# Where the context is rotated: all sixteen tiles inside layer 0's self attention, none inside layer 1's cross attention

## The chip, the core and the metric

The kernel runs on one core of one Trainium2 chip. The metric is the device time of one execution in microseconds (us). The core has a matrix engine (PE), three engines for elementwise work (DVE, ACT, POOL), and a queue, SP, that here issues nearly all DMA transfers. The engines run their own instruction streams in order and wait for one another by semaphores.

## The reference, cut to what matters

The program is a two-layer perceiver on 64 batches of 32 latents of width 256, all in fp32, with a context of 64 x 257 x 64. Each layer is cross attention, self attention and a feed-forward block, with residuals:

```python
x = x + L0_xattn(ln(x), ctx)     # stage A, causal, first 32 context rows
x = x + L0_attn(ln(x))           # stage B, 16 heads of 128, cosine similarity
x = x + L0_ffn(ln(x))            # end of B, and stage C: 4 of 16 blocks for each token
x = x + L1_xattn(ln(x), ctx)     # stage D, all 257 context rows
x = x + L1_attn(ln(x))           # stage E
x = x + L1_ffn(ln(x))            # stage F, 8 experts, one for each token
```

The change concerns what layer 1's cross attention reads. It does not use the context as it came but the context with a rotary position applied:

```python
kv_rope = kv_c * cos[None] + rotate_half(kv_c) * sin[None]     # 64 x 257 x 64
scores  = (q_r of x) . (kv_rope @ W_kr)                        # keys
ctx_c   = softmax(scores) @ kv_rope                            # values
```

kv_rope depends on the inputs alone, so it can be computed at any time before stage D reads it.

## The kernel before

The latents are 2048 rows, held in SBUF as 16 tiles of 128 rows (four batches each). In the profiled execution stage B runs from about 139 to 505 us, C to 636, D to about 985, and E and F to the end.

**The rotation.** One tile of context is four batches. `fetch(t, work)` (L694 to L704) issues ten transfers on SP: two for `rct` (the context turned, L697), four for `rrt` (the same with its halves exchanged, L698 and L699) and four for `rna` (the context not turned, in four runs of rows, L703). `rotate(t, work)` (L706 to L721) does seven POOL multiplications and additions (L710 to L712 on the turned form, L717 to L720 on the other) and three stores on SP: two of `rct` to the DRAM tensor `ctd` (L714), one of `rna` to `nad` (L721). The four SBUF tiles that this needs have one buffer each, so the fetch of the next tile starts when the stores of the last are done. In D, `rotated(t)` (through `d_context`, L1164 and L1165) loads the rotated tile from `ctd` and `nad` as `ct` and `na`, three buffers each.

**Stage B** is a loop of 17 slots, written out by hand. The order of instructions on PE, DVE, ACT and POOL is that of the program text; SP's order is set by the framework's scheduler. Slot t computes similarities of tile t (`similar`, L806 for q.k and L814 for the squared norms, which read `q2b`), the softmax (`scale`, L828 and L830; `power`; `share`, L842 and L843), the values and output projection of tile t-1 (`gather`, L853; `project`, L866), and the queries of later tiles (L775). POOL squares the queries of tile t+1 (`square`, L794, four instructions) and ends the output norm of tile t-1 (`norm_out`, L885 and L886, which wait for DVE's L884). Where this text says that slot t starts, it means the first L806 of tile t. Other pieces are hung into the slots by `at(slot, place, fn)`: keys of the next group, the choice of feed-forward blocks (`choose_best`, L607 to L620, small DVE instructions, in slots 7, 8, 11, 12, 15 and 16), and from slot 11 on the first group of the feed-forward block (`hidden`, L644 to L652; `output`, L657). In every slot SP also writes a padding block (`srt<-pad`, L136).

Before the change `rotate` is called in the even slots, for tiles 0 to 7, each followed by the fetch of the next tile.

**Stage D** is a loop over 64 batches, in this text called blocks. Only PE's order is by hand here; DVE, ACT, POOL and SP follow the framework's scheduler. Block b has scores (L1350), their maximum on DVE (L1358), the exponential on ACT (L1362), the division on DVE (L1371), the turning of the probabilities (L1387, copied by L1393, or by DVE's L1395 every fourth block), and the product with the values (L1410, which reads `na`). DVE's L1373 puts the probabilities of the last context row aside. Every fourth block has a projection (L1426). Tiles 8 to 15 are rotated in blocks 2, 6, ..., 30, in the first half of the loop. So the second half does the same PE work with no rotation beside it.

Of the kernel before, what the change touches and what calls it, by code (L numbers as in the profile page):

```python
# [15 lines left out]
NT = B * S // P  # L16
# [21 lines left out]
def bc(ap, axis, n):  # L38

    shape = list(ap.shape)  # L40
    shape.insert(axis, n)
    return ap.unsqueeze(axis).to_broadcast(shape)
# [3 lines left out]
def perceiver_kernel(ctx: ExitStack, tc: tile.TileContext, a: dict, out: bass.AP):  # L46
# [324 lines left out]
    with tc.tile_pool(name="wA", bufs=2) as work, tc.tile_pool(  # L371
# [59 lines left out]
        def power(t):  # L431
            nc.scalar.activation(sc[t], sc[t], AF.Exp)
# [258 lines left out]
    def fetch(t, work):  # L691

        ct = work.tile([P, 2, NKV], F32, tag="rct", name=f"rct{t}", bufs=1)
        rt = work.tile([P, 2, NKV], F32, tag="rrt", name=f"rrt{t}", bufs=1)  # L694
        for z in range(2):
            src = a["ctxT"][:, 4 * t + 2 * z : 4 * t + 2 * z + 2, :]
            nc.sync.dma_start(ct[64 * z : 64 * z + 64], src)  # L697
            nc.sync.dma_start(rt[64 * z : 64 * z + 32], src[32:64])  # L698
            nc.sync.dma_start(rt[64 * z + 32 : 64 * z + 64], src[0:32])  # L699
        na = work.tile([P, 4, 2, DC], F32, tag="rna", name=f"rna{t}", bufs=1)  # L700
        srcn = a["ctxN"][4 * t : 4 * t + 4].rearrange("b (p c) d -> p b c d", c=3)
        for c, p0, r, k0, n_k in RUNS:
            nc.sync.dma_start(na[p0 : p0 + n_k, :, c, :], srcn[k0 : k0 + n_k, :, r, :])  # L703
        fetched[t] = ct, rt, na  # L704

    def rotate(t, work):  # L706
        ct, rt, na = fetched.pop(t)
        nt = work.tile([P, 4, 2, DC], F32, tag="rnt", name=f"rnt{t}", bufs=1)
        mul = nc.gpsimd.tensor_tensor
        mul(ct, ct, bc(cosT, 1, 2), ALU.mult)  # L710
        mul(rt, rt, bc(sinT, 1, 2), ALU.mult)
        mul(ct, ct, rt, ALU.add)  # L712
        for z in range(2):
            nc.sync.dma_start(  # L714
                ctd[:, 4 * t + 2 * z : 4 * t + 2 * z + 2, :], ct[64 * z : 64 * z + 64]
            )
        mul(nt[:, :, :, 0:32], na[:, :, :, 32:64], bc(sinN[:, :, 0:32], 1, 4), ALU.mult)  # L717
        mul(nt[:, :, :, 32:64], na[:, :, :, 0:32], bc(sinN[:, :, 32:64], 1, 4), ALU.mult)
        mul(na, na, bc(cosN, 1, 4), ALU.mult)
        mul(na, na, nt, ALU.add)  # L720
        nc.sync.dma_start(nad[:, 4 * t : 4 * t + 4], na)  # L721
# [4 lines left out]
    with tc.tile_pool(name="wB", bufs=2) as work, tc.tile_pool(  # L726
# [34 lines left out]
        def query_part(n_):  # L761

            pair, h2 = divmod(n_, NH // 2)
            if pair >= NT // 2:
                return
            if h2 == 0:
                queries[pair] = work.tile([P, NH, 256], F32, tag="qT", name=f"qTb{pair}")
            qT = queries[pair]
            xT = latT[pair // 2]
            c0 = 256 * (pair % 2)  # L770
            q_ps = ps2.tile([P, 2, 256], F32, tag="mm", name=f"qb{pair}_{h2}")
            for hh in range(2):
                h = 2 * h2 + hh
                for k in range(KC):
                    nc.tensor.matmul(  # L775
                        q_ps[:, hh, :],
                        b_q[:, k, h * P : (h + 1) * P],
                        xT[:, k, c0 : c0 + 256],
                        start=(k == 0),
                        stop=(k == KC - 1),  # L780
                    )
            hsl = slice(2 * h2, 2 * h2 + 2)
            nc.scalar.copy(qT[:, hsl, :], q_ps)  # L783
# [42 lines left out]
        def scale(t):  # L826
            s_ps, rq = sims[t]
            nc.vector.reciprocal(rq, rq)  # L828
            pT = sims[t] = work.tile([P, 512], F32, tag="pT", name=f"pTb{t}")
            nc.vector.tensor_tensor(pT, s_ps, rq, ALU.mult)  # L830
# [97 lines left out]
        def ff_late():  # L928
            for fn in late:
                fn()  # L930
            late.clear()
# [32 lines left out]
        for t in range(NT + 1):  # L964


            parts = [AHEAD + 4 * t + z for z in range(4)]

            def place(z):
                if z < 4:  # L970
                    query_part(parts[z])
                for step in steps.get((t, z), ()):
                    step()

            if t < NT:
                similar(t)
            place(0)
            if t > 0:
                gather(t - 1)
            if t < NT:  # L980
                scale(t)
            place(1)
            square(t + 1)
            ff_late()
            place(2)
            if t < NT:
                power(t)
            ff_late()
            place(5)
            if t > 0:  # L990
                project(t - 1)
                norm_stats(t - 1)
            if t < NT:
                share(t)
            place(3)
            ff_late()
            if t > 0:
                norm_out(t - 1)
            if t % 2 == 0 and t < NT:
                rotate(t // 2, work)  # L1000
                if t // 2 + 1 < NT // 2:
                    fetch(t // 2 + 1, work)
            if t == NT - 3:
                rotate_last()
            place(4)
            write_pad(t)
            if t in (2, 4):
                load_c(t // 4)
# [208 lines left out]
    with mbw, wd1:  # L1217
# [3 lines left out]
        with tc.tile_pool(name="wD", bufs=2) as work, tc.tile_pool(  # L1221
# [216 lines left out]
            last_keys(0)  # L1438
            score(0)
            rotated(1)  # L1440
            fetch(NT // 2, work)

            steps, lat = {}, {}
            for g in range(1, NG):
# [22 lines left out]
            for b in range(NB + 2):  # L1467


                if b % 4 == 1 and b // 4 + 2 < NT:  # L1470
                    rotated(b // 4 + 2)
                if b % 4 == 2 and b // 4 < NT // 2:
                    rotate(b // 4 + NT // 2, work)
                    if b // 4 + 1 < NT // 2:
                        fetch(b // 4 + 1 + NT // 2, work)
                if b + 1 < NB:
                    score(b + 1)
                if 1 <= b <= NB:
                    gather(b - 1)
                if b in steps:  # L1480
                    steps[b]()
                if b % 2 == 0 and b // 8 + 1 < NB // 8:
                    query_part(b // 8 + 1, (b % 8) // 2)
                if b >= 5 and (b - 1) % 4 == 0:
                    project((b - 5) // 4)
                if b < NB:
                    turn(b)
                elif b == NB:
                    last_part(NT - 1, ps1.tile([P, 2, 256], F32, tag="o", name="odl"))
                if b == 40:  # L1490
                    nc.gpsimd.tensor_tensor(e_bk, bc(e_b[:, 1], 2, 2), bc(mask2, 1, KC), ALU.mult)
                if b == 16:

                    e_q = wep.tile([P, KC, D], F32, name="e_q")
                    by_pairs(e_q, a["e_wq"])
                    e_k = wep.tile([P, KC, D], F32, name="e_k")
                    for k in range(KC):
                        for z in range(4):
                            o, w = divmod(z, 2)
                            nc.sync.dma_start(  # L1500
                                e_k[:, k, o * P : (o + 1) * P].rearrange(
                                    "p (r w d) -> p w r d", r=4, w=2
                                )[:, w],
                                a["e_wk"][k * P : (k + 1) * P, :].rearrange(
                                    "p (r d) -> p r d", r=4
                                ),
                            )

                    e_b = wep.tile([P, 2, KC], F32, name="e_b")
                    for z, v0 in enumerate((V_BQ, V_BK)):  # L1510
                        for o in range(KC):
                            for r in range(4):
                                p0 = 64 * (r % 2) + 32 * o
                                nc.sync.dma_start(
                                    e_b[32 * r : 32 * r + 32, z, o : o + 1],
                                    a["vecs"][p0 : p0 + 32, v0 + r // 2 : v0 + r // 2 + 1],
                                )
                    e_bk = wep.tile([P, KC, 2], F32, name="e_bk")
                    e_v = wep.tile([P, KC, DC], F32, name="e_v")
                    nc.sync.dma_start(e_v, a["e_wv"].rearrange("(k p) o -> p k o", p=P))  # L1520
                    f_r = wep.tile([P, KC, 8], F32, name="f_r")
                    nc.sync.dma_start(f_r, a["f_wr"].rearrange("(k p) o -> p k o", p=P))
# [673 lines left out]
```

## Time and profile before

| what | value |
|---|---|
| time, median of 3 runs | 1271.13 us (1268.81 to 1275.26) |
| the profiled execution's own time | 1276.62 us, of which the span of its instructions 1274.7 us |
| PE busy | 1188.2 us, 93% |
| DVE busy | 783.9 us, 61% |
| ACT busy | 557.5 us, 44% |
| POOL busy | 374.7 us, 29% |
| mean granted PE clock | 0.946 of full speed |
| DMA | 103.11 MB, mean 81 GB/s |

A busy share is an average over stages. The row of the granted clock tells at what part of full speed PE's clock ran: a matmul that takes 0.2 us at full clock takes 0.4 us at half, and both count as busy. In the lists of instructions, what stands in brackets is how long the engine sat idle before it, and what it waited for.

### The profile page before, as it was taken

The numbers are of one execution on the slowest core, as the hardware profiler recorded it, in microseconds if no ns is written. First come the engines' busy times: TensorE is split into PE (matmuls) and PEld (weight loads), VectorE is DVE, ScalarE is ACT, GpSimd is POOL, SyncE is SP. The second block draws the span as 40 slices with busy tenths as digits, with TensorE's granted clock in tenths as the row PEclk, the third lists the DMA queues.
The fourth block names the chain that finished last, engine by engine and source line by source line (L and its number), as shares of the span: only waits on it lengthen the run. The fifth ranks groups of instructions, "written<-read, shape, count | busy, mean of one in ns | idle before, by whom it ended". The sixth has DMA issues, their size and how long they took to land. (4 is left out here: it accounts for less than half of the span.)

```text
span 1274.7 us, 26240 instructions
## 1 busy us (share of the span) xinstructions
PE 1188.2 (93%) x10187; PEld 834.5 (65%) x10187; DVE 783.9 (61%) x1885; ACT 557.5 (44%) x1305; POOL 374.7 (29%) x472
## 2 busy tenths in 40 slices
PE   8999999999999997999979999999999778789997
PEld 5656767677776565777747766776766455656664
DVE  5776147678768866433286877767676466555333
ACT  2337344464543631222354645665655355331111
POOL 2333334445443631000053444001010356332111
PEclk8889999999999989979999989999999898579999
DMA  5121122433242422912154453111100254211110
GB/s 143 45 69 35 28 75 76 124 118 109 76 142 67 140 86 73 279 39 68 44 142 109 85 139 105 37 46 37 47 9 2 69 167 160 66 38 55 43 32 10
DMA packets 94973, 103.11 MB, mean 81 GB/s; under 512 B 37792, under 2 KB 71329, under 8 KB 94626
## 3 DMA queue, kind: packets, MB, share of 16 engines
q1 hardware_dynamic: 92978, 97.19, 26.9%
q0 software_dynamic: 1872, 4.23, 0.9%
q8 instruction: 82, 1.34, 0.4%
q14 instruction: 41, 0.34, 0.1%
HBM read 69.45 MB, written 32.85 MB: 80 GB/s over the span
## 5 line engine op out<-in xcount | busy, mean ns | idle before, releaser
L1362 ACT ACTIVATE pp<-Sd,nm 128x257 f32<-128x257 f32 x256 | 118.0, 474 | 78.3 <-DVE nm L1358 73.7
L775 PE MATMUL qb<-xT_b,b_q 128*128 128x256 f32 x512 | 123.5, 390 | 0.0
L775 PEld LDWEIGHTS qb<-xT_b,b_q 128*128 128x128 f32 x512 | 96.4, 193 | 39.9 <-issue 19.8
L866 PE MATMUL yb<-b_o,oTb 128*128 128x256 f32 x512 | 115.9, 385 | 0.0
L866 PEld LDWEIGHTS yb<-b_o,oTb 128*128 128x128 f32 x512 | 98.3, 194 | 14.2 <-issue 1.0
L1371 DVE TENSOR_TENSOR pp<-pp,rd 128x514 f32<-128x514 f32 x128 | 98.4, 769 | 2.1
L1358 DVE TENSOR_REDUCE nm<-Sd 128x2 f32<-128x514 f32 x128 | 83.0, 686 | 20.0 <-PE Sd L1350 20.0
L1393 ACT COPY pTd<-pt 128x512 f32<-128x512 f32 x112 | 61.5, 599 | 56.6 <-PE pt L1387 56.6
L1410 PE MATMUL od<-pTd,na 128*64 128x256 f32 x480 | 67.0, 401 | 13.0 <-issue 11.7
L794 POOL TENSOR_TENSOR q2b<-qTb 128x512 f32<-128x512 f32 x64 | 65.4, 1050 | 28.4 <-ACT qTb L783 17.1
L1350 PE MATMUL Sd<-ct,qTd 64*128 64x257 f32 x480 | 68.9, 404 | 0.5 <-ACT pp L1362 0.4
L783 ACT COPY qTb<-qb 128x512 f32<-128x512 f32 x64 | 37.4, 584 | 72.4 <-PE qb L775 70.8
L885 POOL TENSOR_TENSOR ynb<-ynb,vec 128x256 f32<-128x256 f32 x16 | 11.6, 725 | 191.2 <-DVE ynb L884 191.2
L1387 PE MATMUL pt<-cst,pp 128*128 128x128 f32 x512 | 66.9, 274 | 0.0
L1387 PEld LDWEIGHTS pt<-cst,pp 128*128 128x128 f32 x512 | 58.9, 141 | 9.8 <-issue 5.4
L1426 PE MATMUL yd<-d_n,co 128*128 128x256 f32 x256 | 65.2, 412 | 0.0
L1148 PE MATMUL qd<-xT_d,d_m 128*128 128x256 f32 x256 | 64.5, 395 | 0.2 <-ACT xT_d L242 0.2
L828 DVE RECIPROCAL rqb<-rqb 128x512 f32<-128x512 f32 x16 | 53.5, 3343 | 17.8 <-ACT rqb L823 17.8
L657 PE MATMUL yc<-c,hc 128*128 128x256 f32 x256 | 60.5, 393 | 2.7 <-DVE hc L652 2.7
L1426 PEld LDWEIGHTS yd<-d_n,co 128*128 128x128 f32 x256 | 51.3, 206 | 14.0 <-issue 6.5
L657 PEld LDWEIGHTS yc<-c,hc 128*128 128x128 f32 x256 | 49.9, 198 | 12.4 <-DVE hc L652 3.5
L1148 PEld LDWEIGHTS qd<-xT_d,d_m 128*128 128x128 f32 x256 | 46.8, 192 | 17.0 <-issue 6.0
(389 smaller groups left out, 2384.8 us busy)
## 6 DMA issues: line engine op xcount, KB each, us to landing
srt<-pad SPq DMA_DIRECT2D x17, 1040.0 KB
mb<-maskd SPq DMA_DIRECT2D x64, 128.0 KB
ct<-ctd SPq DMA_DIRECT2D x30, 257.0 KB
rct<-in_ctxT_dram SPq DMA_DIRECT2D x32, 128.5 KB
rrt<-in_ctxT_dram SPq DMA_DIRECT2D x64, 64.2 KB
ctd<-rct SPq DMA_DIRECT2D x32, 128.5 KB
nad<-rna SPq DMA_DIRECT2D x16, 256.0 KB
fw<-in_f_wg_dram SPq DMA_DIRECT2D x8, 512.0 KB
```

The source lines that it names most:

```text
L657: nc.tensor.matmul(y_ps, hs[f][:, i * P : (i + 1) * P], c_2[:, f, :], start=(f == 0), stop=(f == 7),)
L775: nc.tensor.matmul(q_ps[:, hh, :], b_q[:, k, h * P : (h + 1) * P], xT[:, k, c0 : c0 + 256], start=(k == 0), stop=(k == KC - 1),)
L794: nc.gpsimd.tensor_tensor(q2[:, 4 * h4 : 4 * h4 + 4, :], q, q, ALU.mult)
L866: nc.tensor.matmul(y_ps, oT[:, h, :], b_o[:, h, :], start=(h == 0), stop=(h == NH - 1))
L1148: nc.tensor.matmul(q_ps[:, r, :], m[:, k, pr * P : (pr + 1) * P], xT[:, k, c0 : c0 + 256], start=(k == 0), stop=(k == KC - 1),)
L1350: nc.tensor.matmul(s_ps[:, hh, :NKV], qT[hs, b % 8, 4 * u : 4 * u + 4, :], ct[hs, b % 4, :], start=True, stop=True,)
L1358: nc.vector.tensor_reduce(nm, s_ps[:, :, :NKV], AX.X, ALU.max, negate=True)
L1362: nc.scalar.activation(pp[:, hh, :], s_ps[:, hh, :NKV], AF.Exp, bias=nm[:, hh : hh + 1], accum_out=sd[:, hh : hh + 1],)
L1371: nc.vector.tensor_tensor(pp, pp, bc(rd, 2, NKV), ALU.mult)
L1387: nc.tensor.transpose(pt[:, hh * 256 + u * P : hh * 256 + u * P + P], probs[b][:, u, hh, c * P : (c + 1) * P], ident,)
L1410: nc.tensor.matmul(o_ps[64 * hh : 64 * hh + 64, 0, :], na[:, j, c, :], pT[:, c, hh * 256 : (hh + 1) * 256], start=(c == 0), stop=(c == 1),)
L1426: nc.tensor.matmul(y_ps, co[:, pr, :], n[:, pr, :], start=(pr == 0), stop=False)
```

## The change

`rotate` is called in every slot of stage B, for tiles 0 to 15, and `fetch` for the next tile after it. The calls in stage D go away, with the fetch ahead of its loop. Nothing else is edited. The instruction orders of PE, DVE and ACT are the same in both programs; on POOL the rotations of tiles 8 to 15 move from D into B, and SP's transfers move with them.

```diff
@@ stage B, end of slot t @@
-            if t % 2 == 0 and t < NT:
-                rotate(t // 2, work)
-                if t // 2 + 1 < NT // 2:
-                    fetch(t // 2 + 1, work)
+            if t < NT:
+                rotate(t, work)
+            if t + 1 < NT:
+                fetch(t + 1, work)
@@ stage D, ahead of the loop @@
             rotated(1)
-            fetch(NT // 2, work)
@@ stage D, block b @@
-                if b % 4 == 2 and b // 4 < NT // 2:
-                    rotate(b // 4 + NT // 2, work)
-                    if b // 4 + 1 < NT // 2:
-                        fetch(b // 4 + 1 + NT // 2, work)
```

## The prediction

> **What bounds the kernel now.** I read the page first, for the bound and the clock.
>
> ```profile
> PE 1188.2 (93%) x10187; PEld 834.5 (65%) x10187; DVE 783.9 (61%) x1885; ACT 557.5 (44%) x1305; POOL 374.7 (29%) x472
> PEclk8889999999999989979999989999999898579999
> ```
>
> PE is the bound in B and in D; what counts is where PE stops or runs at less than its full clock. The edit touches B and D, so next I cut D into stretches of four blocks (columns: length in us, busy time of PE, its weight loads, DVE, ACT, POOL, granted clock, DMA share, GB/s).
>
> ```profile
> 655.50:683.40 27.90, 23.88 (x143) 16.58 (x142) 20.76 (x41) 14.08 (x48) 16.78 (x14) 0.88 0.53 135
> 683.40:704.40 21.00, 20.63 (x144) 15.20 (x142) 16.62 (x42) 12.81 (x43) 6.71 (x6) 1.00 0.38 102
> 704.40:725.30 20.90, 20.46 (x140) 14.64 (x139) 18.47 (x38) 12.43 (x42) 9.98 (x8) 1.00 0.47 101
> 745.40:771.90 26.50, 23.78 (x145) 17.03 (x144) 19.77 (x40) 13.20 (x44) 16.68 (x14) 0.87 0.46 121
> 771.90:796.20 24.30, 22.27 (x145) 16.33 (x144) 19.71 (x41) 12.77 (x43) 8.54 (x7) 0.93 0.43 117
> 836.40:857.00 20.60, 20.60 (x145) 15.12 (x144) 15.13 (x38) 13.31 (x44) 0.00 (x0) 1.00 0.18 42
> 857.00:879.00 22.00, 20.52 (x143) 15.16 (x142) 16.57 (x39) 12.71 (x43) 3.68 (x4) 1.00 0.16 40
> 879.00:899.10 20.10, 20.10 (x139) 14.64 (x138) 14.31 (x36) 12.41 (x42) 0.00 (x0) 1.00 0.12 31
> ```
>
> All have nearly the same PE work. Without POOL work four blocks take 20.1 us, or 20.6 with the turning of a normed group; the first five rows, with the rotations, take up to 27.9, at a lower clock. The timeline of the first shows why (start, duration, engine).
>
> ```profile
> 665.70 0.58 SPq L1165 DMA_DIRECT2D na<-nad  x1
> 666.27 1.57 DVE L1371 TENSOR_TENSOR pp<-pp,rd 128x514 f32<-128x514 f32 x1
> 667.37 1.59 POOL L720 TENSOR_TENSOR rna<-rna,rnt 128x512 f32<-128x512 f32 x1
> 667.88 1.10 DVE L1373 TENSOR_TENSOR plast<-pp,ones 128x4 f32<-128x4 f32 x1
> 668.90 0.68 DVE L1395 COPY pTd<-pt 128x512 f32<-128x512 f32 x1
> 669.88 1.97 PE L1410 MATMUL od<-pTd,na 128*64 128x256 f32 x8 [3.35 <-issue]
> ```
>
> L1371 takes 1.57 us, and 0.69 when POOL is idle; L1373 takes 1.10 for a 128x4 operation that is 0.16 elsewhere. So DVE's copy L1395 ends at 669.58, the `na` load, issued late on SP among the rotation's transfers, has just landed, and PE stood still for 3.35 us. The same stop is at 757.96 (2.39 us) and 783.65 (2.04 us).
>
> Last, one slot of B that has a rotation today:
>
> ```profile
> 214.09 0.72 POOL L885 TENSOR_TENSOR ynb<-ynb,vec 128x256 f32<-128x256 f32 x1 [13.07 <-DVE ynb L884]
> 215.58 1.28 POOL L710 TENSOR_TENSOR rct<-rct,cst 128x514 f32<-128x514 f32 x1
> 223.37 4.03 POOL L794 TENSOR_TENSOR q2b<-qTb 128x512 f32<-128x512 f32 x4
> 229.70 1.04 PE L814 MATMUL ssb<-q2b,ones 128*32 128x512 f32 x8
> ```
>
> POOL rotates from 215.58 to 223.4, squares until 227.40, and PE wants the squares at 229.70: 2.3 us to spare, no stop. That is the slot which the change makes of every slot.
>
> **The change part by part.**
>
> *D loses eight rotations.* Each stretch is set against its like without rotation. 655.5 to 683.4: 27.9 - 20.6 = 7.3. 745.4 to 771.9: 26.5 - 20.6 = 5.9. 683.4 to 704.4: 0.4. 704.4 to 725.3: 20.9 - 20.1 = 0.8. 771.9 to 796.2 also has four L194 norms on DVE, as has 857 to 879, which stops for 1.5 us without a rotation; between 20.6 and 22.0, I take 21.3: 24.3 - 21.3 = 3.0. The stretch before them, 636.6 to 655.5, begins with the filling of the pipeline (PE waits 3.14 us for ACT's first exponentials) and gets nothing. Sum 17.4 us; from 16.7 to 18.7, the upper end with 20.6 in the last case and 0.6 in the first stretch. What is late next there is nothing but PE.
>
> Of these 17.4, stops are 3.35 + 2.39 + 2.04 = 7.8 us, and the low clock is 27.9 x 0.12 + 26.5 x 0.13 + 24.3 x 0.07 = 8.5 us; the small rest is two stretches at full clock. After a stop PE runs at half clock: 16 projection matmuls behind each stop take 5.4 to 5.9 us, and 3.7 behind the 1.48 us stop at 868. [...] The rows at 757 and 784 show the fall after 2.39 and 2.04 us, while a stop of 2.48 us at 396.7 in B left the clock at 1.00. The trace decides for this execution, but which stop is punished is partly luck[...].
>
> *B gains eight rotations on POOL*, run about 5 us after the start of slots 2, 4, ..., 16. One is 1.28 + 1.18 + 1.27 + 0.73 + 0.73 + 1.27 + 1.27 = 7.7 us. POOL's chain in a slot becomes 1.4 (norm) + 7.7 + 4.0 (squares) = 13.2 us in slots of 18 to 22 us. In the even slots the squares are ready 10.2 to 12.1 us ahead of L814; that leaves 2.5 to 4.4 us, as in the odd slots today (2.3 to 6.3). Cost 0, hidden by those slacks. If they are used up, L814 stops PE and everything behind it in PE's queue. The next norm_out on POOL waits for L884 of the next slot in any case.
>
> *SP.* Each rotation moves 3 stores and 10 loads, 104 transfers in all. In the slot above SP issues the store of `rna` at 223.44 and the ten loads until 230.04; such loads land some 2 us after their issue (in D, L717 waited until 784.47 for loads issued by 782.46). The turned form is there by 229, the rest by 232; the next rotation could start at 234.7 and needs the rest at 238.4. Over 5 us to spare, cost 0. Moved past on SP: the padding stores keep their place ahead of the rotation's stores; mask loads `mb` for the second feed-forward group move from 466 to about 473 and are wanted after 503; layer 1's weights start at 507.8, and the last rotation's store comes at about 494. In D, the 35 small loads of stage E's weights move ahead, to about 650 to 670, and tile 4's context behind them is wanted at 725: 0.
>
> *DVE beside POOL in B.* [...] The row first: in slot 7, beside the squares, L609, L610, L616 and L618 of `choose_best` take 0.71 to 0.96 us, and 0.22 once POOL is done. Yet the large instructions L828, L830 and L858 keep their 3.34, 0.69 and 0.69 us beside POOL. [...] By the rows, one wait is 0.6 us, so 9 x 0.6 = 5.4, cut short when POOL goes idle (326.7 in slot 8, 410.8 in slot 12): DVE is late by 0.8 and 1.5 us at yb's norm L168, and L853 has 0 to 1.3 us of slack. PE stops 0.3 us in each, say 0.6. Slot 6 (six small norm operations), 14 (three L652) and 16 (the last choice, ready by 497 and wanted at 499.1) have more DVE idle time than they lose. With 0.4 for a stop of a kind that I don't see, B costs 1.0 us[...].
>
> Sum for the profiled execution: 1276.62 - 17.4 + 1.0 = 1260.2. It ran 5.5 us above the median of the runs. As half of what is saved is lost clock, which varies, I put 2 us of those 5.5 among the savings: 16.4 - 2.0 = 14.4, and 1271.1 - 14.4 = 1256.7, say 1256.5.
>
> **The rivals.**
>
> *B gives back a part.* [...] PE stops for 1.5 us in slots 8, 12 and 16, and two stops halve the clock for a window of 3.4 us (1.7 each): 8 us. 1271.1 - 15 + 8 = 1264. For it: the stop of 2.48 us at 396.7 is already DVE's lateness in slot 11. Against: DVE idle time of 3.7 us in slots 8 and 12.
>
> *D's stops stay.* They would be the norms' DVE work, not the rotation; only the shares of the two stretches at full clock and a little more go: 1271.1 - 2 = 1269. Against: blocks from 836 on have the same norms and stop once, for 1.5 us.
>
> *Slower: POOL is late for the squares.* POOL's chain needs 2.5 us more than I think, by late fetches with one slot of lead instead of two. Then L814 stops PE by about 2 us in the seven slots that wait for such squares, each with a half-clock window of 3.4 to 6.8 us (2.5 lost): 7 x 4.5 = 31.5, less 16: 1287. It decides from a landing 5 us later than the 2 us above. Against: stores and loads of B land in time today with the padding of 1 MB beside them.
>
> **How the numbers follow.** Likeliest, 0.70: 1256.5, with its own range 1251 to 1262. B gives back a part 0.18, D's stops stay 0.07, POOL late 0.05. The range 1249 to 1266 reaches down to the 18.7 us of the upper sum and the spread of single runs (2 to 4 us)[...]. What can be told from no change is about 0.5%, 6.4 us, so faster is below 1264.8: 0.70 + 0.15 + 0.01 = 0.86; same 0.09; slower 0.05.
>
> **What would show it.** In D after, POOL is empty of rotation, the stretches of four blocks take 20.1 to 21.5 us at clock 1.00, L1371 is near 0.70 in the mean, and no L1410 waits over 1.5 us. In B every slot shows L710 about 5 us in, with no wait for DMA; L814 never waits for POOL; slots 8 and 12 show `choose_best` stretched and L853 late by less than 1 us. I am wrong if L814 waits for L794, L710 waits for `rct` or `rrt` in B, new half-clock windows appear between 300 and 450, or D keeps its 26 us stretches.

## The result, and the profile after

The changed kernel takes 1259.68 us (median of 8 runs, 1254.64 to 1262.62), the kernel before 1270.64 us (8 runs, 1265.97 to 1278.98). The ratio is 0.9898, 95% interval 0.9878 to 0.9919: about 1.0% faster, 11 us by the medians and 13 us by the ratio. The two profiled executions took 1276.62 and 1262.62 us.

By stages, measured between the first and last matmuls of each on PE, the two profiled executions differ so:

| stage | before | after | difference |
|---|---|---|---|
| A (to the first L806) | 155.0 | 152.0 | -3.0, same code |
| B (to the last L866) | 343.9 | 348.6 | +4.7 |
| C (to the first L1350) | 137.7 | 138.9 | +1.3, same code |
| D (to the last projection) | 353.5 | 336.5 | -17.0 |
| E and F | 284.6 | 284.7 | 0, same code |

Two groups of D from the page of the kernel before (busy us and mean ns, then the idle time before them), and from the page of the changed kernel the first row of busy times, the granted clock in 40 slices and the same groups:

```profile
L1371 DVE TENSOR_TENSOR pp<-pp,rd 128x514 f32<-128x514 f32 x128 | 98.4, 769 | 2.1
L1410 PE MATMUL od<-pTd,na 128*64 128x256 f32 x480 | 67.0, 401 | 13.0 <-issue 11.7
```

```profile
PE 1186.6 (94%) x10187; PEld 832.7 (66%) x10187; DVE 775.8 (62%) x1885; ACT 557.9 (44%) x1305; POOL 368.6 (29%) x472
PEclk9989989999998989998989999999999888689999
L1371 DVE TENSOR_TENSOR pp<-pp,rd 128x514 f32<-128x514 f32 x128 | 89.0, 695 | 2.1
L1410 PE MATMUL od<-pTd,na 128*64 128x256 f32 x480 | 65.3, 392 | 5.6 <-issue 4.3
```

The totals hardly move; the place of the work does. L1371 falls from 769 to 695 ns in the mean, and L1410's idle time from 13.0 to 5.6 us. Next, D of the changed kernel in stretches of four blocks (columns as in the prediction).

```profile
658.90:679.40 20.50, 20.50 (x143) 15.11 (x142) 15.33 (x39) 12.87 (x43) 0.20 (x1) 1.00 0.19 38
679.40:700.40 21.00, 20.63 (x143) 15.20 (x142) 16.19 (x41) 12.81 (x43) 0.00 (x0) 1.00 0.16 41
700.40:720.50 20.10, 20.10 (x139) 14.64 (x138) 14.81 (x37) 12.41 (x42) 0.00 (x0) 1.00 0.17 45
740.60:761.20 20.60, 20.60 (x145) 15.09 (x144) 15.77 (x40) 13.32 (x44) 0.00 (x0) 1.00 0.18 45
761.20:782.20 21.00, 20.62 (x145) 15.21 (x144) 16.20 (x41) 12.80 (x43) 0.00 (x0) 1.00 0.16 42
```

These are the stretches that took 27.9, 21.0, 20.9, 26.5 and 24.3 us. All five now run at full clock. The block that had the stop of 3.35 us, in the timeline of the changed kernel:

```profile
666.56 0.69 DVE L1371 TENSOR_TENSOR pp<-pp,rd 128x514 f32<-128x514 f32 x1
667.29 0.16 DVE L1373 TENSOR_TENSOR plast<-pp,ones 128x4 f32<-128x4 f32 x1
667.43 0.69 DVE L1395 COPY pTd<-pt 128x512 f32<-128x512 f32 x1
668.58 1.08 PE L1410 MATMUL od<-pTd,na 128*64 128x256 f32 x8
```

L1371 and L1373 take their undisturbed 0.69 and 0.16 us, DVE's copy ends at 668.12, and L1410 has no idle time in brackets: the copy is done before PE wants it.

In B the group of L710 shows all sixteen rotations and what POOL waited for ahead of them (last column); PE's waits in B follow (total us, times, longest).

```profile
L710 POOL TENSOR_TENSOR rct<-rct,cst 128x514 f32<-128x514 f32 x16 | 20.5, 1279 | 0.0
...
PE yc L657 <- DVE hc L652: 2.7, 2, 1.7
PE avb L853 <- DVE pTb L843: 2.5, 1, 2.5
```

No rotation waited for a transfer, and PE never waits for POOL. The two stops that are listed exist in the kernel before as well, with the same lengths. The squares end 2.0 to 5.8 us ahead of L814 in slots 3 to 15.

### The profile page after: what moved, and what is told of

The parts are those of the page before. It is cut to its first block, busy times and chain, and to the rows that moved or that the text cites. A ratio compares the mean times of both kernels' runs of the same rounds, so it can differ in the third digit from the quotient of the medians.

```text
span 1260.7 us, 26257 instructions
## 1 busy us (share of the span) xinstructions
PE 1186.6 (94%) x10187; PEld 832.7 (66%) x10187; DVE 775.8 (62%) x1885; ACT 557.9 (44%) x1305; POOL 368.6 (29%) x472
## 5 line engine op out<-in xcount | busy, mean ns | idle before, releaser
L775 PEld LDWEIGHTS qb<-xT_b,b_q 128*128 128x128 f32 x512 | 97.4, 195 | 41.4 <-issue 20.9
L866 PE MATMUL yb<-b_o,oTb 128*128 128x256 f32 x512 | 116.4, 386 | 0.0
L866 PEld LDWEIGHTS yb<-b_o,oTb 128*128 128x128 f32 x512 | 98.6, 194 | 14.4 <-issue 0.7
L1371 DVE TENSOR_TENSOR pp<-pp,rd 128x514 f32<-128x514 f32 x128 | 89.0, 695 | 2.1
L1410 PE MATMUL od<-pTd,na 128*64 128x256 f32 x480 | 65.3, 392 | 5.6 <-issue 4.3
L1350 PE MATMUL Sd<-ct,qTd 64*128 64x257 f32 x480 | 68.3, 403 | 0.0
L1426 PE MATMUL yd<-d_n,co 128*128 128x256 f32 x256 | 59.5, 386 | 0.0
L842 DVE RECIPROCAL rdb<-denb 128x512 f32<-128x512 f32 x16 | 53.7, 3355 | 6.7 <-PE denb L840 6.5
L1426 PEld LDWEIGHTS yd<-d_n,co 128*128 128x128 f32 x256 | 47.3, 190 | 11.6 <-issue 5.8
```

Of the source, the lines that this page charges most:

```text
L775: nc.tensor.matmul(q_ps[:, hh, :], b_q[:, k, h * P : (h + 1) * P], xT[:, k, c0 : c0 + 256], start=(k == 0), stop=(k == KC - 1),)
L866: nc.tensor.matmul(y_ps, oT[:, h, :], b_o[:, h, :], start=(h == 0), stop=(h == NH - 1))
L1350: nc.tensor.matmul(s_ps[:, hh, :NKV], qT[hs, b % 8, 4 * u : 4 * u + 4, :], ct[hs, b % 4, :], start=True, stop=True,)
L1371: nc.vector.tensor_tensor(pp, pp, bc(rd, 2, NKV), ALU.mult)
L1410: nc.tensor.matmul(o_ps[64 * hh : 64 * hh + 64, 0, :], na[:, j, c, :], pT[:, c, hh * 256 : (hh + 1) * 256], start=(c == 0), stop=(c == 1),)
L1426: nc.tensor.matmul(y_ps, co[:, pr, :], n[:, pr, :], start=(pr == 0), stop=False)
```

## The experiments

There are twelve runs, each beside the kernel before on the same chip; ratios are to that kernel, with their 95% intervals. To set one against the changed kernel, its ratio is divided by 0.9898.

**D's part alone** (e1)

```diff
 B: rotations of tiles 0 to 7 in the even slots, as before
-                if b % 4 == 2 and b // 4 < NT // 2:
-                    rotate(b // 4 + NT // 2, work)
...
-                nc.sync.dma_start(ct[64 * z : 64 * z + 64], ctd[:, 4 * t : 4 * t + 4, :])
+                nc.sync.dma_start(
+                    ct[64 * z : 64 * z + 64], ctd[:, 4 * (t % 8) : 4 * (t % 8) + 4, :]
+                )
... (na likewise)
```

> Stage B as in the kernel before (rotations in the even slots only), stage D without any rotation: tiles 8 to 15 are never rotated, and D loads tile t mod 8 in their place, so their own context is left out. This is D's part of the change alone. If D's gain is as summed and B's rotations cost about nothing: 13 to 17 us below the kernel before, and the same as the changed kernel within 2 us. If B gives something back (its stage was 4.7 us longer in the profile of after): up to 5 us further below than the changed kernel. Stage D in its profile near 336 us in both cases.

Measured: 1255.35 us, ratio 0.9887 (0.9860 to 0.9913), so 14.4 us below the kernel before. Stage D 335.2 us. The interval covers the changed kernel's ratio: within it, all of the gain is D's.

**B's part alone** (e2)

```diff
-            if t % 2 == 0 and t < NT:
-                rotate(t // 2, work)
+            if t < NT:
+                rotate(t, work)
... (fetch likewise)
 D: fetch and rotate of tiles 8 to 15 stay, as before
```

> All sixteen rotations in B as in the changed kernel, and tiles 8 to 15 rotated a second time in D, with all their transfers, as before. This is B's part of the change alone, a price without its return. If B's rotations are hidden: the kernel before within 2 us. If B gives back what the profile of after seems to show: 3 to 6 us above the kernel before. Stage D near 353 us in both cases.

Measured: 1270.26 us, ratio 0.9997 (0.9976 to 1.0019). Sixteen rotations in B in place of eight cost nothing that can be seen, 3 us at most one way or the other. Stage B in its profile was 341.1 us, and 341.1 us in e1 with eight rotations; D 349.7 us. So the 4.7 us by which B was longer in the profile of after isn't the change. They are a matter of the clock, taken up below. The 349.7 us of D matter as well: it has the same rotations as the kernel before, whose profile shows 353.5.

**POOL's instructions alone in D** (e3), and **the transfers alone in D** (e4), both added to the changed kernel

```diff
 e3, at b % 4 == 2, b < 32, on the tiles that D has loaded (src, na), into scratch:
+    mul(ct, src[:, 0:2], bc(cosT, 1, 2), ALU.mult)
+    mul(rt, src[:, 2:4], bc(sinT, 1, 2), ALU.mult)
+    mul(ct, ct, rt, ALU.add)
...
 e4, at the same places:
+    nc.sync.dma_start(ctx2[...], ct[64 * z : 64 * z + 64])   # z = 0, 1
+    nc.sync.dma_start(nax2[...], na)
+    fetch(b // 4 + 1 + NT // 2, work)
... (and the first fetch, ahead of the loop)
```

> The changed kernel, and in D, at the places where the kernel before rotates, the seven POOL instructions of a rotation in their old shapes, reading the context tiles that D has loaded and writing scratch; no transfers added. If POOL's instructions hold DVE up [...], D's loss comes back: 10 to 17 us above the changed kernel, L1371 at 0.8 us or more in the first half of D, stops of 2 to 3.4 us ahead of L1410. If the loss was in SP's queue (the late load of na among the rotation's transfers): within 2 us of the changed kernel.

> The changed kernel, and in D the transfers of a rotation alone: ten loads and three stores (to scratch in DRAM) for each of eight tiles at the places where the kernel before has them, with no POOL instruction. If POOL holding DVE up was the loss: within 3 us of the changed kernel. If SP's queue and the late load of na were: 10 to 17 us above the changed kernel, with L1410 waiting for na.

Measured: e3 1281.5 us, ratio 1.0078 (1.0054 to 1.0103); e4 1256.44 us, ratio 0.9893 (0.9866 to 0.9921). The transfers cost nothing that can be seen. In e4 the same stretches of D move over 140 GB/s and run at full clock:

```profile
647.00:667.50 20.50, 20.50 (x144) 15.09 (x142) 15.01 (x37) 12.87 (x43) 0.00 (x0) 1.00 0.51 141
667.50:688.00 20.50, 20.13 (x141) 14.77 (x140) 16.18 (x41) 12.31 (x43) 0.00 (x0) 1.00 0.52 142
```

POOL's instructions bring the whole loss back and more: 1.0078 / 0.9898 is 1.8%, some 23 us, where 10 to 17 were expected. (L1371 takes 928 ns in the first half of D, 853 in the kernel before.) Stage D took 354.8 us in its profile, 18.3 more than in the changed kernel; C, whose code is the same, took 5.3 us more, which POOL's instructions in D do not explain; C had eight half-clock windows there, and six in the changed kernel. One block of e3 in the timeline:

```profile
718.24 1.61 POOL L1451 TENSOR_TENSOR sct<-sct,srt 128x514 f32<-128x514 f32 x1
718.82 1.58 DVE L1371 TENSOR_TENSOR pp<-pp,rd 128x514 f32<-128x514 f32 x1
...
723.08 0.75 POOL L1452 TENSOR_TENSOR snt<-na,sinN 128x256 f32<-128x256 f32 x1 [3.23 <-DMA na<-nad]
...
723.34 1.03 DVE L1371 TENSOR_TENSOR pp<-pp,rd 128x514 f32<-128x514 f32 x1
...
724.41 0.57 DVE L1373 TENSOR_TENSOR plast<-pp,ones 128x4 f32<-128x4 f32 x1
724.90 0.68 DVE L1395 COPY pTd<-pt 128x512 f32<-128x512 f32 x1
...
725.88 1.08 PE L1410 MATMUL od<-pTd,na 128*64 128x256 f32 x8 [1.61 <-issue]
```

L1410 reads the `na` of tile 3 here, whose load went out at 653.93 and which POOL had read at 670.09; the one that POOL waits for until 723.08 is tile 5's. So it isn't `na` that L1410 waits for. DVE's L1371 and L1373 are stretched beside POOL, the copy L1395 behind them ends at 725.58, and PE has stood still for 1.61 us. L1395, which reads PSUM, keeps its 0.68 us. The L1410 of every fourth block from 4 to 24, those whose last turned probabilities DVE copies, has such a stop, of 1.6 to 2.8 us, and each time it starts 0.3 us after the end of L1395.

That settles the rival that these two runs were made for, late loads in SP's queue: it falls. The transfers of e4 never wait for POOL, so e4 alone can't show a queue held up by stores that do; but e3 has the stops without any added transfer, and in the kernel before the loads of `na` for the three blocks that stop (tiles 1, 5 and 6) went out at 639.35, 710.50 and 738.69, at least 30 us ahead of each stop's end.

**Which instructions hold DVE up** (e10: POOL's seven with one input each; e11: the kernel before with DVE's division in two one-input instructions)

```diff
 e10, in e3:
-    mul(ct, src[:, 0:2], bc(cosT, 1, 2), ALU.mult)
+    nc.gpsimd.tensor_scalar(ct, src[:, 0:2], 1.5, None, ALU.mult)
...
 e11, in the kernel before, L1371:
-    nc.vector.tensor_tensor(pp, pp, bc(rd, 2, NKV), ALU.mult)
+    for hh in range(2):
+        nc.vector.tensor_scalar(pp[:, hh, :], pp[:, hh, :], rd[:, hh : hh + 1], None, ALU.mult)
```

> The run that put POOL's seven instructions alone into D, with each of them made a one-input multiplication by a constant, same outputs in shape, results unused. If DVE is held up for as long as POOL works, whatever POOL reads: the loss shrinks only with POOL's busy time. If it takes a POOL instruction with two inputs: most of the loss goes, within 5 us of the changed kernel.

> The kernel before, rotations in D and all, with the division L1371 written as two DVE instructions of one SBUF input and a scalar for each row, 128x257 each, in place of one instruction with two SBUF inputs of 128x514. If POOL holds up only DVE instructions with two SBUF inputs: D's stops go or shrink, 7 to 15 us below the kernel before, less what 128 more instructions cost on DVE [...]. If POOL holds DVE up whatever it reads: the same as the kernel before within 3 us, or slower by the added instructions.

Measured: e10 1259.35 us, ratio 0.9910 (0.9874 to 0.9946), as the changed kernel; e11 1267.45 us, ratio 0.9985 (0.9968 to 1.0001), as the kernel before, or 2 us less. The DVE groups of L1371 between 640 and 800 us, first in e3, then in e10:

```profile
L1371 DVE TENSOR_TENSOR pp<-pp,rd 128x514 f32<-128x514 f32 x54 | 50.1, 928 | 0.9
```

```profile
L1371 DVE TENSOR_TENSOR pp<-pp,rd 128x514 f32<-128x514 f32 x62 | 45.4, 733 | 1.0
```

With one input POOL's instructions are even longer (1.52 to 1.73 us at 128x512 and 128x514, where the two-input ones take 1.31 to 1.54 in e3), and yet DVE is hardly slowed (733 ns, for 690 in the changed kernel) and D takes 337.9 us. So here it was POOL's two-input instructions that held DVE up by much. The edit changes the kind of instruction (`tensor_tensor` to `tensor_scalar`) with the number of inputs; the two are not told apart here. On DVE's side one input did not save it: in e11 the group of the new division, beside the rotations (660 to 790 us), and in the second half (800 to 960 us):

```profile
L1372 DVE TENSOR_SCALAR pp<-pp,rd 128x257 f32<-128x257 f32 x94 | 45.4, 524 | 0.7
...
L1372 DVE TENSOR_SCALAR pp<-pp,rd 128x257 f32<-128x257 f32 x123 | 39.3, 362 | 1.0
```

It takes 362 ns in the second half and 524 in the mean beside the rotations. Without POOL the two halves cost hardly more than the one instruction did (2 x 362 against 700 ns), so the added instructions are not what eats the gain. The D of e11 was 345.0 us, between before and after, but stops of 1.7 to 2.1 us stayed in three blocks, and the total says that this is no remedy.

**How much slack B has** (e5, e6: one and three more POOL multiplications of 128x512 after each rotation)

```diff
         mul(na, na, nt, ALU.add)
+        for z in range(1):        # e6: range(3)
+            rx = work.tile([P, 4, 2, DC], F32, tag="rx", name=f"rx{t}_{z}", bufs=1)
+            mul(rx, na, bc(cosN, 1, 4), ALU.mult)
```

> The changed kernel with one more POOL multiplication (128x512, 1.27 us by L719's row) after each of the sixteen rotations in B, its result unused. The squares have 2.0 to 5.5 us to spare ahead of L814, so 0.8 us is left in the tightest slot. If that slack is what hides the rotations: the changed kernel within 2 us, no stop at L814. If POOL in B slows DVE enough to cost time already (the rival that B gives back): 2 to 5 us above the changed kernel.

> The changed kernel with three more POOL multiplications (3.8 us) after each rotation in B. The seven slots whose squares have 1.7 to 2.9 us to spare (3, 4, 5, 9, 13, 14, 15) then miss L814 by 0.9 to 2.1 us, the others keep 0.3 to 2 us. If slack is the point from which the slower rival decides: about 10 us of stops at L814 that wait for L794, and with half clock behind some of them 10 to 27 us above the changed kernel. If other slack exists behind L814 (the softmax of the tile ahead of it): under 5 us.

Measured: e5 1262.26 us (four runs), ratio 0.9893 (0.9865 to 0.9921), no different from the changed kernel; 0.75 us is left ahead of L814 in the tightest slot. e6 1272.88 us, ratio 1.0004 (0.9989 to 1.0019), 1.1% or some 13 us above the changed kernel. PE's waits at L853 in B of e5, then those at L853 and L814 in e6 (in the changed kernel L853 waits once, for 2.5 us, and L814 never):

```profile
PE avb L853 <- DVE pTb L843: 4.9, 3, 3.3
```

```profile
PE avb L853 <- DVE pTb L843: 7.4, 2, 5.2
PE ssb L814 <- POOL q2b L794: 6.9, 6, 2.7
```

In e6 L814 waits for the squares, 6.9 us in all, and L853 waits 4.9 us more than in the changed kernel. So the slack at L814 is one thing that hides the rotations: 1.3 us more leave some of it, and with 3.8 us more, half as much again as the rotation's own 7.7 us, the whole gain is gone. But it isn't the first to give way. In e5, where L814 never waits, L853 already waits 2.4 us more than in the changed kernel, in slots 4, 8 and 12, because DVE's small instructions are stretched for longer beside POOL and L843 comes late (ahead of the stop at 233.4, L183 takes 0.96 us, and 0.17 in the changed kernel). These 2.4 us are too few to be seen in the total.

**Two stops of B that were there before** (e7: layer 0's feed-forward norm one slot earlier; e8: every rotation but the last one slot earlier, so that none runs in slot 15; e9 and e12: both)

```diff
 e7
-        at(11, 5, lambda: ff.update(xn=ln_group(0, "c", act=True)))
+        at(10, 5, lambda: ff.update(xn=ln_group(0, "c", act=True)))
 e8, at the end of slot t, in place of the calls there
+            for u in (0, 1) if t == 0 else (t + 1,) if t < NT - 2 else (t,) if t == NT - 1 else ():
+                rotate(u, work)
+                if u + 1 < NT:
+                    fetch(u + 1, work)
```

> The changed kernel with layer 0's feed-forward norm of the first four tiles (L194 on DVE) hung into slot 10 in place of slot 11, where it makes DVE's L843 late and PE stops for 2.48 us at L853 in slot 12, in all kernels so far. If DVE has the idle time in slot 10: that stop goes, 2 to 4 us below the changed kernel (2.5 of stop, and the half clock of 3.4 to 6.8 us that sometimes follows). If it is as late in slot 11 as it was in slot 12: the stop moves by a slot, and the time is the same within 2 us.

> The changed kernel with the rotations one slot earlier: tiles 0 and 1 one after the other, then one in each slot, none in slot 15, the last in slot 16. In slot 15 POOL's rotation runs beside DVE's L652 (two inputs from SBUF), and PE's L657 waits 1.7 and 1.0 us for it, followed by 3.4 to 10.2 us of half clock, in the kernel before as well. If POOL holding DVE up makes that stop: it goes, 3 to 7 us below the changed kernel. If L652 is late by ACT's L650 alone: same within 2 us.

> The changed kernel with both edits of the last two runs: the norm in slot 10, the rotations one slot earlier and none in slot 15. If the two stops are independent, the gains add: some 6 to 7 us and some 8 us below the changed kernel by their medians, 1243 to 1247 us. If much of either was the clock's chance: 1247 to 1252.

> The kernel with both stops of B removed, run again. Its stage B was 335.6 us, shorter than with either edit alone (340.2 and 338.1), but its stage C, whose code is untouched, took 145.5 us against 138.9 and 140.5, with PE at half clock in eight windows in a row in which it is fully busy. If those windows are the clock's own state in some executions: C near 138 to 140 us this time and 1245 to 1250 us in all. If the edits bring them about: C near 145 us and 1253 us again.

| run | median us | ratio | stage B | stage C |
|---|---|---|---|---|
| e7 | 1252.80 | 0.9818 (0.9784 to 0.9852) | 340.2 | 138.9 |
| e8 | 1249.02 | 0.9822 (0.9789 to 0.9855) | 338.1 | 140.5 |
| e9, both | 1253.17 | 0.9878 (0.9848 to 0.9908) | 335.6 | 145.5 |
| e12, both again | 1247.72 | 0.9802 (0.9765 to 0.9840) | 335.6 | 142.1 |

In e7 PE's wait at L853 is gone from the list, and slot 12 takes 19.33 us where it took 21.88 before and 24.97 in the profile of after. In e8 PE's waits between 440 and 480 us are:

```profile
PE yc L657 <- DVE hc L652: 1.4, 1, 1.4
```

One stop in place of two, 1.4 us for 2.7, and no half clock behind it in that profile. So POOL beside L652 made about half of it; the other half stays without POOL. Each edit alone is 7 to 11 us below the changed kernel, by medians or ratios, where 2 to 4 (e7) and 3 to 7 (e8) were expected. That is more than the stops themselves; half-clock windows in B went from 7 in the profile of after to 3 and 1. Both together make B shortest, and the two takes of the same kernel differ by 5.4 us in their medians, 1.2% and 2.0% below the kernel before, with intervals that do not meet; e9 lies outside both of its expected ranges, e12 in its first. In their profiles C differs by 3.4 us, which is two half-clock windows (e9 has three and five of them in C, with four at full clock between, not eight in a row; e12 has two and four). So the edits don't bring a fixed 145 us about. All four are clearly below the kernel before. Against the changed kernel it is less sure: one kernel came out 0.8% apart in two takes, and 0.8% is what e7 and e8 are below it. Their profiles show that the stops went; how much that is worth, and which edit or pair is best, the runs don't tell.

## Why the prediction was right, point by point

*D's loss of rotations.* Predicted 17.4 us, measured 17.0 for the whole of D in the profiled executions, and 17.4 in the five stretches. The stretches came out at 20.5, 21.0, 20.1, 20.6 and 21.0 us, for forecasts of 20.6, 20.6, 20.1, 20.6 and 21.3. The 0.4 of the second stretch did not come: its stop of 0.37 us is still there, so it was not the rotation's; the last stretch gave 0.3 more than forecast. The mechanism (POOL holds DVE up, DVE's copy is late, PE stops) is shown by e3 and e4, each part by itself: with POOL's instructions alone L1371 takes 928 ns and PE stops for 1.6 to 2.8 us, with the transfers alone L1371 keeps 689 ns and the stretches full clock. The prediction misread one line: the `na` load issued at 665.70 is tile 3's, which L1410 first reads at 714.45. The block that stopped reads tile 1's, from 639.35. The amount was partly luck: e2's D, with the same rotations, took 349.7 us in its profile, 13.2 more than the D of after, with stops of 2.19, 2.18 and 1.96 us in place of 3.35, 2.39 and 2.04 and two half-clock windows behind them in place of five.

*B's gain of rotations.* Predicted 1.0 us, of which 0.3 us each were stops in slots 8 and 12. e2 measures 0 within 3 us, and the two stops didn't come. Slot 8 is 19.3 us in the kernel before, in e2 and in after; slot 12 is 21.88 us in the kernel before, 21.89 in e2, 21.87 in e4. DVE's `choose_best` was stretched, as foreseen (L609 1.27 us, L620 1.07 us in slot 12), but DVE's idle time took it up. The squares' slack came out at 2.0 to 5.8 us; foreseen were 2.5 to 4.4 in the slots that gain a rotation and 2.3 to 6.3 in the others. e5 shows how near the other limit was: the lateness of DVE at L853, which the prediction priced, sets in with 1.3 us more.

*The 4.7 us of B in the profile of after* was not in the sum, and it would have looked like the rival "B gives back a part". 3.1 us of it are in slot 12. The stop there is 2.48 us in both executions, for the same reason; once the clock fell behind it and once it didn't. PE's busy time (second column) and the clock (third column from the end) in stretches of 3.41 us around it, before and then after:

```profile
392.22:395.63 3.41, 2.02 (x12) 1.44 (x8) 3.34 (x4) 3.41 (x8) 0.00 (x0) 1.00 0.00 0
395.63:399.04 3.41, 2.32 (x14) 1.43 (x15) 3.12 (x8) 1.09 (x3) 1.49 (x3) 1.00 0.07 23
```

```profile
391.00:394.41 3.41, 1.37 (x7) 0.86 (x5) 3.38 (x2) 2.79 (x7) 0.00 (x0) 1.00 0.00 0
394.41:397.82 3.41, 2.96 (x10) 1.35 (x11) 2.20 (x7) 0.76 (x2) 2.13 (x3) 0.50 0.27 92
```

In every profile all falls of the clock start on one grid of 3.41 us. In the kernel before the stop lies across a line of that grid and leaves PE busy for 2.02 and 2.32 us of two windows; in after, most of it lies in one window, PE is busy for 1.37 us, and the next two windows run at half clock. In the kernel before, one matmul of L1426 starts 0.216 us after the other at full clock and 0.427 us at half (medians), so by estimate a half-clock window loses 3.41 x (1 - 0.216 / 0.427) = 1.7 us. The rest of the 4.7 us is clock too: B has seven half-clock windows in after and four in the kernel before, against two in e1 and in e2 (341.1 us both) and one in e4 (339.4 us).

Over B and D (140 to 480 and 635 to 975 us) of all fourteen profiles, the windows at full clock divide like this:

| PE busy in the window | windows | followed by half clock |
|---|---|---|
| under 0.41 | 38 | 38 |
| 0.41 to 0.49 | 14 | 7 |
| 0.49 to 0.70 | 55 | 0 |
| 0.70 to 0.80 | 43 | 4, all at the stop of slot 15 |
| above | 2557 | 0 |

So in these profiles a stop cost clock when it took somewhat over half of one window, 1.7 to 2.0 us, and where the grid lies against the program differs from execution to execution. Four falls in 150 windows don't fit; each comes right behind a window in which PE was busy for 0.50. The prediction took the low clock from the trace, and for that profile this was right: D's gain was summed to 17.4 us, and 17.4 came. The prediction's "partly luck" now has a cause.

*From the profiled execution to the median.* I took 2 us off for an execution that was 5.5 us above its median, and forecast a gain of 14.4 us. Measured are 13.0 by the ratio (10.3 to 15.5 by its interval) and 14.4 in e1, but 11.0 by the two medians. The kernels that have the D of after or nearly so lie at 0.9887 (e1), 0.9893 (e4 and e5) and 0.9910 (e10). The predicted 1256.5 is 3.2 us below the median of 1259.7, inside its own range. The upper end of the wide range, 1266, was an estimate.

*The rivals.* The three stops of 1.5 us behind "B gives back a part" were an estimate; e2 puts B's cost at 0 within 3 us. "D's stops stay" is ruled out by D's 336.5 us. "POOL is late for the squares" didn't come about here. Its price was right in kind and too high in size: it put 2.5 us more in POOL's chain at 31.5 us (2 us of stop in seven slots, each with half clock behind it). e5 shows that 1.3 us more cost nothing that the total tells, and e6 that 3.8 us more cost 13: the stops at L814 were 6.9 us in six slots, four of them under 1 us, and B had eight half-clock windows, one more than in after.

## What to carry to other kernels

An idle POOL did not make elementwise work on it free: with two inputs it stretched DVE's division beside it (L1371 from 690 ns in the changed kernel to 928 in e3, in the mean), and what mattered was whether somebody waited for DVE at that place. Put such work where DVE has idle time and where POOL's own consumer has slack, and measure both first. Here 2.0 us were left at L814 at the tightest; 1.3 us more did not show in the total but did at L853, behind DVE, and 3.8 us more took the gain. When one stage of one profile grows by a few us, look at whether its stops are new or only their clock, before blaming the edit.

## What the runs showed of the hardware that was not expected

- On the grid of 3.41 us, a window in B and D with PE busy for less than 0.41 of it was always followed by half clock (38 of 38), one between 0.49 and 0.70 never (0 of 55).
- POOL with one input for each instruction left DVE nearly alone (L1371 733 ns, against 928 beside two-input instructions), though POOL's instructions were longer. A one-input DVE instruction from SBUF to SBUF was still stretched beside two-input POOL ones (524 ns for 362).
- Stage C has half clock of another kind: 1 to 5 windows of it in a row begin some 40 us into the stage, 60 to 67 us into it, or at both, with PE busy for all of the windows ahead. All 25 of these falls, in fourteen profiles, come during matmuls that stream 64 columns or fewer, or at their very end: 11 of them 3.2 to 5.7 us after the start of L1053, 14 of them 1.1 to 3.4 us after the start of L1066, ahead of which runs L583. In e9, the matmuls and then the windows ahead of the two falls and behind them:

```profile
528.11 7.70 PE L1053 MATMUL t1p<-d_kr,d_rt 64*96 64x64 f32 x64
552.45 1.85 PE L583 MATMUL lpc<-c_r,xTr 128*128 128x16 f32 x16
554.15 12.94 PE L1066 MATMUL t2p<-d_t,d_at 96*128 96x64 f32 x64
```

```profile
527.91:531.32 3.41, 3.41 (x41) 3.24 (x39) 2.82 (x7) 0.95 (x2) 0.00 (x0) 1.00 1.05 261
531.32:534.73 3.41, 3.41 (x24) 3.41 (x24) 1.48 (x5) 0.63 (x2) 0.00 (x0) 0.50 0.78 221
551.80:555.21 3.41, 3.41 (x28) 2.95 (x26) 1.32 (x4) 1.88 (x2) 0.00 (x0) 1.00 0.02 5
555.21:558.62 3.41, 3.41 (x19) 3.41 (x18) 0.31 (x2) 0.26 (x1) 0.00 (x0) 0.50 0.00 0
```

So PE can be busy for a whole window and still lose its clock in the next. That it is these matmuls that do it is not shown, since no run changed them. How many such windows fall into C differs, and with the same code C took 137.7 us at the least, with 4 half-clock windows in all (the kernel before), and 145.5 us at the most, with 9 (e9).
